# Packed small matmuls in the prologue and the channel gate, and the last image's convolutions in two parts, in a fused attention and convolution kernel

## The chip, the cores and the metric

The kernel runs on one core of a Trainium2 chip. The metric is the device time of one execution in microseconds (us). The core has five engines that run side by side and meet at semaphores: TensorE (PE in the profile; its weight loads are PEld), VectorE (DVE), ScalarE (ACT), GpSimd (POOL) and SyncE (SP, which here issues most DMA transfers). The kernel before takes 3579.54 us, the median of three runs (3570.65 to 3580.26).

## The reference

Two images x of 256 channels by 64 by 64 pixels, all in float32, go through two layers. Cut to what matters:

```python
# layer 0: full attention over 4096 tokens, 8 heads of 32 channels
m = resize(mask, (B, 1, 64, 64), "bilinear")
q, k, v = proj(Wq, bq) / sqrt(32), proj(Wk, bk), proj(Wv, bv)
fuse = softmax(q @ k.T) @ v                        # per image and head
hybrid = conv1x1(concat([x, fuse]), Wf, bf)
x = hybrid * m + x * (1 - m)

# layer 1
a = relu(x @ ca_w1 + ca_b1) @ ca_w2 + ca_b2        # channel gate: 256 -> 64 -> 256
x = x * sigmoid(a)
x = x + window_attention(x)                        # 8 by 8 windows, 4 heads of 64
x = shuffle_channels(x, 4)
y = relu(bn1(conv7x7(x, sa_w1, groups=64)))        # 256 -> 64 channels
y = bn2(conv7x7(y, sa_w2, groups=64))              # 64 -> 256 channels
out = x * sigmoid(y)
```

## The kernel before

**Prologue.** For every image and every chunk of 512 tokens (16 chunks in all), PE computes q, k and v, which go to DRAM. It also sums the squares of q and k per head. Their maxima give a bound on the scores, by which the kernel chooses at run time whether softmax may go without subtracting the row maximum ("arm a", the one that runs here) or not ("arm b"). Each sum of squares is a matmul with 32 columns of weights. These matmuls stand right behind the projection whose squares they sum:

```python
norms = ps1.tile([P, CH], F32, tag="av", name=f"nrm_{b}_{c}")
for i, (n, w, eng) in enumerate((("q", wq, 0), ("k", wk, 1))):
    s = psum2(f"{n}0_{b}_{c}")
    ...                                   # 4 matmuls of 128x128 weights by 512 tokens (L156)
    for g in range(KC):
        nc.vector.tensor_scalar_add(t[:, g, :], s[:, g, :], bt[:, g : g + 1])
        nc.scalar.activation(sq[:, g, :], s[:, g, :], AF.Square, bias=bt[:, g : g + 1])
    for g in range(KC):
        r = 64 * i + 32 * g
        nc.tensor.matmul(norms[r : r + 32, :], headsum, sq[:, g, :], start=True, stop=True)
...                                       # then v (L185) and the maximum of norms
```

GpSimd meanwhile builds banded weights for the two 7x7 convolutions in DRAM (`w1_s`, `w2_s`), zeroing them and then writing their diagonals.

**Attention loop.** It has 1024 slots: image, chunk of 512 queries, half of the heads, block of 128 keys. In each slot PE makes scores for four heads in four row tiles (L484), ACT takes the exponential (L492), DVE adds it to a running sum (L508) and PE multiplies by v in four column tiles (L506). The denominators (`dna`, L523) are four neighbouring column tiles too. Keys and values are loaded every four slots, two pieces ahead.

Once a chunk is done, its further path (fusion, channel gate, window attention) runs as a "stage" of 15 steps, one every fourth slot of the next chunk. The channel gate is two of those steps:

```python
for kc in range(KC):
    nc.tensor.matmul(s[0:CR, 0, :], cw1[:, kc, :], x1[:, kc, :], start=(kc == 0), stop=(kc == KC - 1))
gt = gp.tile([CR, CH], F32, tag="g", name=f"g{tag}")
nc.scalar.activation(gt, s[0:CR, 0, :], AF.Relu, bias=cb1)
yield
s = psum2(f"ca2{tag}")
for oc in range(KC):
    nc.tensor.matmul(s[:, oc, :], cw2[:, oc * P : (oc + 1) * P], gt, start=True, stop=True)
```

**Convolutions.** An image's convolutions start once its eighth chunk is stored in DRAM (`x_s`). The rows are cut into three overlapping blocks of 30; the partition dimension holds 4 channels x 30 rows. A unit is `UG = 4` channels of each of four quarters, so there are 16 units. All three blocks are side by side in one matmul: 3 x 64 = 192 columns. Per unit each convolution has 28 matmuls (two records each in the profile).

```python
conv_after = {(b, NCHUNK - 1): (0, 1, 2) for b in range(B)}
...
def load_w(u):                                     # banded weights, 448 KB each
    for ws, d, i in ((w1s, w1_s, 1), (w2s, w2_s, 2)):
        t = wsp.tile([P, 32, UW], F32, tag="w", name=f"w{i}{tag}_{u}")
        nc.sync.dma_start(t, d[u])
        ws[u] = t

def load_x(u):                                     # 4 loads per block
    if u >= NU:
        return
    x = xs[u] = xcs[u % len(xcs)]                  # four buffers
    for n, blk in enumerate(blocks):
        r = BLOCKS[blk][0]
        for q in range(4):
            ...
            nc.sync.dma_start(x[4 + q : 4 + 4 * RB : 4, n], x_s[b][r : r + RB, gs, :])
...
load_w(0)
load_w(1)
yield
for u in range(len(xcs)):
    load_x(u)
yield
conv1(0)
yield
for u in range(NU):
    conv1(u + 1)                                   # PE (L783), then Relu on ACT
    yield
    z = conv2(u)                                   # PE (L804), then sigmoid on ACT
    yield
    gate(u, z)                                     # DVE (L826), then stores
    if u + 2 < NU:
        load_w(u + 2)
    load_x(u + len(xcs))
    yield
```

The first image's convolutions run beside the second image's attention, one step every fourth slot (`if i % 4 == 2: run_convs()`). Those of the last image have nothing left to run beside; they make the tail. Stores there are shared between GpSimd's and ScalarE's queues.

Of the kernel before, what the change touches and what calls it, by code (L numbers as in the profile page):

```python
# [10 lines left out]
F32 = mybir.dt.float32  # L11
# [28 lines left out]
RB = 30  # L40
BLOCKS = ((0, 0, 24), (17, 24, 40), (34, 40, 64))
NG = C // 4
UG = 4
UQ = UG // 4
NU = NG // UG
UW = UG * KS
EPS = 1e-5
# [6 lines left out]
def conv_seq_kernel(ctx: ExitStack, tc: tile.TileContext, a, out):  # L54
# [24 lines left out]


    xcs, ycs = [], []
    for u in range(4):
        t = const.tile([P, len(BLOCKS), UG, WP], F32, name=f"xc{u}")
        nc.gpsimd.memset(t, 0.0)
        nc.gpsimd.memset(t[0:1], 1.0)
        xcs.append(t)
        t = const.tile([P, UQ, len(BLOCKS), WP], F32, name=f"yc{u}")
        nc.gpsimd.memset(t, 0.0)
        ycs.append(t)

# [32 lines left out]
    with (  # L123
# [19 lines left out]
        for b in range(B):  # L143
            src = a["x"][b].rearrange("(k p) h w -> p k (h w)", p=P)
            for c in range(NCHUNK):
                x = x0.tile([P, KC, CH], F32, tag="x", name=f"x0_{b}_{c}")
                nc.sync.dma_start(x, src[:, :, c * CH : (c + 1) * CH])
                norms = ps1.tile([P, CH], F32, tag="av", name=f"nrm_{b}_{c}")
                for i, (n, w, eng) in enumerate((("q", wq, 0), ("k", wk, 1))):
                    s = psum2(f"{n}0_{b}_{c}")  # L150
                    for g in range(KC):
                        for kc in range(KC):
                            rhs = x[:, kc, :]
                            if n == "q":
                                rhs = rhs.rearrange("p (r w c) -> p w r c", r=WS, w=NW)
                            nc.tensor.matmul(  # L156
                                s[:, g, :],
                                w[:, kc, g * P : (g + 1) * P],
                                rhs,
                                start=(kc == 0),  # L160
                                stop=(kc == KC - 1),
                            )
                    t = st0.tile([P, KC, CH], F32, tag=n, name=f"{n}st_{b}_{c}")
                    sq = st0.tile([P, KC, CH], F32, tag="sq", name=f"{n}sq_{b}_{c}")
                    bt = bias["b" + n]
                    for g in range(KC):
                        nc.vector.tensor_scalar_add(t[:, g, :], s[:, g, :], bt[:, g : g + 1])  # L167
                        nc.scalar.activation(
                            sq[:, g, :], s[:, g, :], AF.Square, bias=bt[:, g : g + 1]
                        )  # L170
                    for g in range(KC):
                        r = 64 * i + 32 * g
                        nc.tensor.matmul(
                            norms[r : r + 32, :], headsum, sq[:, g, :], start=True, stop=True
                        )
                    if n == "q":
                        nc.sync.dma_start(q_s[b, c], t.rearrange("p g n -> p (g n)"))
                    else:
                        for g in range(KC):
                            nc.sync.dma_start(k_s[b, g, c], t[:, g, :])  # L180
                s = psum2(f"v0_{b}_{c}")
                sv = s.rearrange("p a (t o) -> p (a t) o", t=2)
                for m in range(4):
                    for kc in range(KC):
                        nc.tensor.matmul(  # L185
                            sv[:, m, :],
                            x[:, kc, m * P : (m + 1) * P],
                            wv[:, kc, :],
                            start=(kc == 0),
                            stop=(kc == KC - 1),  # L190
                        )
                v = st0.tile([P, KC, 4, P], F32, tag="v", name=f"vst_{b}_{c}")
                nc.scalar.copy(
                    v.rearrange("p g m d -> p m g d"),
                    sv.rearrange("p m (g d) -> p m g d", g=KC),
                )
                for g in range(KC):
                    nc.sync.dma_start(v_s[b, g, c], v[:, g].rearrange("p m d -> p (m d)"))
                i = b * NCHUNK + c
                nc.vector.tensor_reduce(nm[:, i : i + 1], norms, AX.X, ALU.max)  # L200
# [19 lines left out]
    wo = load("out_w", [P, KC, C], a["out_w"].rearrange("(k p) o -> p k o", p=P), nc.scalar)  # L220
    bo = load("out_b", [P, KC], a["out_b"], nc.scalar)
    cw1 = load("ca_w1", [P, KC, CR], a["ca_w1"].rearrange("(k p) o -> p k o", p=P), nc.scalar)
    cb1 = load("ca_b1", [CR, 1], a["ca_b1"], nc.scalar)
    cw2 = load("ca_w2", [CR, C], a["ca_w2"], nc.scalar)
    cb2 = load("ca_b2", [P, KC], a["ca_b2"], nc.scalar)


# [51 lines left out]
        "bn2", bn2.rearrange("p h q (s k) -> p (h q) s k", k=2)  # L279
    )  # L280
    raw2 = cwp.tile([rows, 16, 4, KS], F32, name="raw2")
    m2 = cwp.tile([rows, NU, 4, UQ, KS], F32, name="m2")
    nc.gpsimd.memset(m2, 0.0)
    src = a["sa_w2"].rearrange("(h q j) k (y x) -> h k j y q x", h=2, j=4, y=KS)
    for i in range(4):
# [4 lines left out]
    for i in range(4):  # L290
        h, k = i % 2, i // 2
        v = sc2.rearrange("p (h q) k -> p h q k", h=2)[:, h, :, k]
        nc.vector.tensor_mul(
            m2[0:nd, :, i],
            raw2[0:nd, :, i, :].rearrange("p (u q) x -> p u q x", q=UQ),
            v[0:nd].rearrange("p (u q) -> p u q", q=UQ).unsqueeze(3).to_broadcast(
                [nd, NU, UQ, KS]
            ),
        )
        v = sh2.rearrange("p (h q) k -> p h q k", h=2)[:, h, :, k]  # L300
        nc.vector.tensor_copy(
            m2[32:36, :, i, :, PAD], v[32:36].rearrange("p (u q) -> p u q", q=UQ)
        )

    zero = cwp.tile([P, 32 * UW], F32, name="zero")
# [70 lines left out]
    def pipeline(arm, shifted, pools):  # L376
# [191 lines left out]
        def stage(b, c):  # L568
# [33 lines left out]
            if nxt[0] < B:  # L602
                load_x(*nxt)
            yield
            s = psum2(f"ca1{tag}")
            for kc in range(KC):
                nc.tensor.matmul(  # L607
                    s[0:CR, 0, :], cw1[:, kc, :], x1[:, kc, :], start=(kc == 0), stop=(kc == KC - 1)
                )
            gt = gp.tile([CR, CH], F32, tag="g", name=f"g{tag}")  # L610
            nc.scalar.activation(gt, s[0:CR, 0, :], AF.Relu, bias=cb1)
            yield
            s = psum2(f"ca2{tag}")
            for oc in range(KC):
                nc.tensor.matmul(  # L615
                    s[:, oc, :], cw2[:, oc * P : (oc + 1) * P], gt, start=True, stop=True
                )
            t = gp.tile([P, KC, CH], F32, tag="t", name=f"sg{tag}")
            for oc in range(KC):
                nc.scalar.activation(  # L620
                    t[:, oc, :], s[:, oc, :], AF.Tanh, bias=cb2[:, oc : oc + 1], scale=0.5
                )
            nc.scalar.activation(t, t, AF.Copy, bias=0.5, scale=0.5)
            u = wp.tile([P, KC, CH], F32, tag="u", name=f"u{tag}")
# [121 lines left out]
            if (b, c) in conv_after:  # L746
                convs.append(ahead.pop(0) if ahead else convolve(b, conv_after[b, c]))

        conv_after = {(b, NCHUNK - 1): (0, 1, 2) for b in range(B)}

        def convolve(b, blocks):
# [9 lines left out]
                    ws[u] = t  # L763

            def load_x(u):
                if u >= NU:
                    return
                x = xs[u] = xcs[u % len(xcs)]
                for n, blk in enumerate(blocks):
                    r = BLOCKS[blk][0]  # L770
                    for q in range(4):
# [3 lines left out]
            def conv1(u):  # L775
# [1 line left out]
                    return  # L777
                x, w = xs[u], w1s.pop(u).rearrange("p m (g d) -> p g d m", g=UG)
                s = psum2(f"c1{tag}_{u}")
                for q in range(UQ):  # L780
                    for d in range(KS):
                        for j in range(4):
                            nc.tensor.matmul(  # L783
# [6 lines left out]
                y = ys[u] = ycs[u % 2]  # L790
                nc.scalar.activation(  # L791
                    y[:, :, 0:nb, PAD : PAD + W],
                    s[:, 0:UQ, 0 : nb * W].rearrange("p q (n x) -> p q n x", n=nb),
                    AF.Relu,
                )

            def conv2(u):
                y, w = ys.pop(u), w2s.pop(u).rearrange("p m (i q d) -> p q d (m i)", q=UQ, i=4)
                tiles = [psum2(f"c2{tag}_{u}_{hh}") for hh in range(2)]
                for q in range(UQ):  # L800
                    for d in range(KS):
                        for j in range(4):
                            r = slice(32 * j, 32 * j + 32)
# [4 lines left out]
                                start=(d == 0),  # L808
                                stop=(d == KS - 1),
                            )  # L810
                z = cp.tile([P, UQ, 4, len(BLOCKS) * W], F32, tag="z", name=f"z{tag}_{u}")
                z = z[:, :, :, 0 : nb * W]
                for hh in range(2):
                    nc.scalar.activation(  # L814
                        z[:, :, 2 * hh : 2 * hh + 2, :],
                        tiles[hh][:, :, 0 : UQ * nb * W].rearrange("p j (q f) -> p q j f", q=UQ),
                        AF.Tanh,
                        scale=0.5,
                    )
# [3 lines left out]
            def gate(u, z):  # L823
# [5 lines left out]
                for n, blk in enumerate(blocks):  # L829
                    x0, r0, r1 = BLOCKS[blk]  # L830
                    for i in range(4):
                        p0, p1 = (4 * (r + 1 - x0) + i for r in (r0, r1))

                        eng = nc.scalar if b == B - 1 and i == 3 else nc.gpsimd
                        eng.dma_start(  # L835
                            dst[i, r0:r1, UG * u : UG * u + UG, :], z[p0 : p1 - 3 : 4, :, n, :]
                        )

            load_w(0)
            load_w(1)  # L840
            yield
            for u in range(len(xcs)):
                load_x(u)
            yield
            conv1(0)
            yield
            for u in range(NU):
# [4 lines left out]
                gate(u, z)  # L852
                if u + 2 < NU:
                    load_w(u + 2)
                load_x(u + len(xcs))
                yield

        def run_convs():
# [23 lines left out]
        for i, (b, c, g, m) in enumerate(slots):  # L882
# [14 lines left out]
            run_later()  # L897
            if i % 4 == 0:
                run_stages()
            if i % 4 == 2:  # L900
                run_convs()
        while stages or convs or later:
            now[0] += 1
# [89 lines left out]
```

## Time and profile before

| | |
|---|---|
| Time | 3579.54 us (3570.65 to 3580.26) |
| Span of the profiled execution | 3578.5 us |
| Prologue | 0 to about 256 us |
| Attention loop with stages, convolutions of image 0 beside it from 1877 us on | about 256 to 3290 us |
| Last chunk's stage | to 3350 us |
| Convolutions of image 1 | 3356 to 3578 us |

How to read the profile: a group of instructions is a line with engine, operation, output<-inputs, shapes and count; behind the bar come its busy time in us, the mean duration of one in ns, and the idle time of the engine just ahead of it with what ended that. Records that overlap are counted once in the busy time, so busy time over count can be far below the mean duration where several tiles of the array work at once. A matmul of float32 leaves two records. `32*128` ahead of a shape is the tile of the array in use (rows*columns). The answer by windows gives, for each stretch of time, PE's and PEld's busy time with the number of instructions, the granted clock, the DMA share and GB/s. In the timeline each row has its start, its duration, the engine, what ran, and in brackets the idle time ahead and its releaser. "SPq" rows are the issuing of transfers by SyncE.

### The profile page before, as it was taken

What the parts mean: (1) busy time and instruction counts of PE and PEld (TensorE: products, weight loads), DVE (VectorE), ACT (ScalarE), POOL (GpSimd) and SP (SyncE); (2) the same over time, 40 slices, a digit from 0 to 9 for tenths busy, and PEclk for the clock granted to TensorE, in tenths of its full rate; (3) what the DMA queues carried; (4) which work ended last, traced back from release to release, by engine and by line L of the source; (5) the groups of instructions that cost most, each with busy time, mean ns of one, the idle gap of its engine ahead of it and who ended that gap; (6) DMA issues with size and microseconds to landing.
All of it is one profiled execution on the core that took longest, in us unless ns stands there. A gap on an engine that the chain in (4) does not pass through costs nothing.

```text
span 3578.5 us, 57141 instructions
## 1 busy us (share of the span) xinstructions
PE 3307.4 (92%) x23690; PEld 1145.7 (32%) x23690; DVE 2718.2 (76%) x1775; ACT 2333.0 (65%) x2581; POOL 312.1 (9%) x543
## 2 busy tenths in 40 slices
PE   9999999999999999999998999999999999998565
PEld 3432222222222222223232443334322222222344
DVE  2229989898989898889987786887889898988100
ACT  2228777786868786777775676767677777775111
POOL 6400000000000000000000111121100000000044
PEclk9999999999999999999999999999999999999777
DMA  8942122121212121211223232332212121211143
GB/s 306 201 135 66 48 59 54 54 57 52 59 54 57 48 63 48 60 51 55 56 62 93 78 98 78 97 92 76 61 51 60 48 63 51 54 54 48 48 130 93
DMA packets 159438, 269.94 MB, mean 75 GB/s; under 512 B 41401, under 2 KB 56909, under 8 KB 159169
## 3 DMA queue, kind: packets, MB, share of 16 engines
q1 hardware_dynamic: 130976, 227.93, 22.1%
q0 software_dynamic: 19648, 34.71, 4.0%
q10 hardware_dynamic: 8544, 3.55, 0.4%
q8 instruction: 189, 3.10, 0.4%
q14 instruction: 81, 0.66, 0.1%
HBM read 208.49 MB, written 60.65 MB: 75 GB/s over the span
## 4 chain that ended last, share of the span: by engine, by line
PE 49%; DVE 18%; issue 17%; ACT 3%; SPq 3%; DMA 2%; POOL 0%; DVEq 0%; ACTq 0%; POOLq 0%
PE sa L484 20%; PE ava L506 16%; DVE suma L508 13%; PE qka L633 3%; PE c2a L804 3%; SPq L773 3%; PE c1a L783 2%; ACT ea L492 2%; PE opa L725 1%; PE vwa L650 1%; DVE rda L529 1%; PE ca2a L615 1%; PE ca1a L607 1%; PE oa L708 1%; DVE pbd L689 1%
## 5 line engine op out<-in xcount | busy, mean ns | idle before, releaser
L508 DVE TENSOR_TENSOR suma<-suma,ea 128x2048 f32<-128x2048 f32 x960 | 2199.9, 2292 | 312.9 <-ACT ea L492 235.5
L492 ACT ACTIVATE ea<-sa 128x1024 f32<-128x1024 f32 x2048 | 1985.2, 1023 | 444.5 <-PE sa L484 307.4
L484 PE MATMUL sa<-qa,ka 32*128 32x512 f32 x8192 | 1336.5, 649 | 88.4 <-ACT ea L492 41.3
L506 PE MATMUL ava<-ea,va 128*32 128x512 f32 x8192 | 1111.0, 614 | 0.0
L484 PEld LDWEIGHTS sa<-qa,ka 32*128 32x128 f32 x8192 | 434.1, 186 | 929.4 <-issue 494.4
L506 PEld LDWEIGHTS ava<-ea,va 128*32 128x32 f32 x8192 | 162.6, 109 | 793.5 <-issue 790.3
L835 POOL DMA_DIRECT2D out_dram<-za x336 | 187.6, 566 | 669.7 <-ACT ea L492 458.1
L740 POOL DMA_DIRECT2D xs<-xo x32 | 28.5, 895 | 2310.6 <-DVE xo L735 2309.2
L783 PE MATMUL c1a<-xc,w1a 128*32 128x192 f32 x1792 | 107.9, 406 | 84.7 <-DMA xc<-xs 25.1
L826 DVE TENSOR_TENSOR za<-za,xc 128x768 f32<-128x768 f32 x32 | 30.6, 957 | 199.2 <-ACT za L820 142.6
L633 PE MATMUL qka<-ua,qkv_w 128*128 128x512 f32 x256 | 130.5, 634 | 28.6 <-ACT qka L641 24.9
L783 PEld LDWEIGHTS c1a<-xc,w1a 128*32 128x32 f32 x1792 | 80.8, 151 | 114.2 <-issue 97.0
L804 PE MATMUL c2a<-yc,w2a 32*128 32x192 f32 x1792 | 116.3, 403 | 0.1
L804 PEld LDWEIGHTS c2a<-yc,w2a 32*128 32x128 f32 x1792 | 108.5, 321 | 20.5 <-issue 17.6
L641 ACT ACTIVATE qka<-qka,qkv_b 128x512 f32<-128x512 f32 x64 | 44.0, 687 | 108.8 <-PE qka L633 107.6
L791 ACT ACTIVATE yc<-c1a 128x192 f32<-128x192 f32 x32 | 10.6, 332 | 155.3 <-PE c1a L783 136.9
L529 DVE RECIPROCAL rda<-rda 128x512 f32<-128x512 f32 x32 | 107.1, 3346 | 2.8 <-ACT rda L526 2.8
L814 ACT ACTIVATE za<-c2a 128x384 f32<-128x384 f32 x64 | 27.9, 488 | 94.8 <-PE c2a L804 89.1
L508 DVE TENSOR_TENSOR suma<-ea,ea 128x2048 f32<-128x2048 f32 x32 | 73.1, 2285 | 18.3 <-ACT ea L492 18.3
L633 PEld LDWEIGHTS qka<-ua,qkv_w 128*128 128x128 f32 x256 | 44.8, 195 | 114.6 <-issue 57.9
L167 DVE TENSOR_SCALAR qst<-q,bq 128x512 f32<-128x512 f32 x32 | 24.0, 751 | 70.8 <-PE q L156 58.5
L725 PE MATMUL opa<-ota,out_w 128*128 128x512 f32 x128 | 63.5, 619 | 13.3 <-ACT ya L732 12.4
(124 smaller groups left out, 1634.7 us busy)
## 6 DMA issues: line engine op xcount, KB each, us to landing
ka<-ks SPq DMA_DIRECT2D x256, 256.0 KB
va<-vs SPq DMA_DIRECT2D x256, 256.0 KB
w1a<-w1s SPq DMA_DIRECT2D x32, 448.0 KB
w2a<-w2s SPq DMA_DIRECT2D x32, 448.0 KB
xc<-xs SPq DMA_DIRECT2D x384, 32.8 KB
xs<-xo POOLq DMA_DIRECT2D x32, 280.0 KB, 7.0
x<-in_x_dram SPq DMA_DIRECT2D x16, 512.0 KB
ks<-kst SPq DMA_DIRECT2D x32, 256.0 KB
```

Source lines behind the costliest of these rows:

```text
L484: nc.tensor.matmul(o, k[r, cols], q[r, g, :], start=True, stop=not shifted)
L492: nc.scalar.activation(e[:, 2 * hh : 2 * hh + 2, :], tiles[hh], AF.Exp, scale=SCALE0)
L506: nc.tensor.matmul(av[r, :], v[:, m % PB, r], e[:, j, :], start=start, stop=stop)
L508: nc.vector.tensor_add(total, first[0] if m == 1 else total, e)
L529: nc.vector.reciprocal(rd, rd)
L633: nc.tensor.matmul(s[:, j, :], wqkv[:, kc, o : o + P], u[:, kc, :], start=(kc == 0), stop=(kc == KC - 1),)
L641: nc.scalar.activation(qk[:, n, :], s[:, j, :], AF.Identity, bias=bqkv[:, n : n + 1])
L725: nc.tensor.matmul(s[:, oc, :], wo[:, kc, oc * P : (oc + 1) * P], ot[:, kc, :], start=(kc == 0), stop=(kc == KC - 1),)
L773: nc.sync.dma_start(x[4 + q : 4 + 4 * RB : 4, n], x_s[b][r : r + RB, gs, :])
L783: nc.tensor.matmul(s[32 * j : 32 * j + 32, q, 0 : nb * W], w[:, 4 * q + j, d, :], x[:, 0:nb, 4 * q + j, d : d + W], start=(d == 0), stop=( ...
L804: nc.tensor.matmul(tiles[j // 2][:, j % 2, q * nb * W : (q + 1) * nb * W], w[r, q, d], y[r, q, 0:nb, d : d + W], start=(d == 0), stop=(d = ...
L835: eng.dma_start(dst[i, r0:r1, UG * u : UG * u + UG, :], z[p0 : p1 - 3 : 4, :, n, :])
```

## The change

Three parts. The sums of squares are collected and issued as four neighbouring column tiles of 32, after the chunk's v projection. The channel gate works on two halves of the 512 tokens at once: its first matmul (64 output channels) in two column tiles, its second (64 input channels) in two row tiles, so that both halves of the array have work. And the convolutions are arranged anew, with the last image's split: the two upper row blocks start after chunk 5 and run beside the attention of the last chunk, with steps every second slot, and only the third block remains for the tail. In this arrangement a unit has 8 channels of each quarter (8 units), tiles have two buffers instead of four, and all stores of results go through GpSimd.

```diff
-UG = 4
-UQ = UG // 4
+UG = 8
...
-    for u in range(4):
+    for u in range(2):
         t = const.tile([P, len(BLOCKS), UG, WP], F32, name=f"xc{u}")
...
-                    for g in range(KC):
-                        r = 64 * i + 32 * g
-                        nc.tensor.matmul(
-                            norms[r : r + 32, :], headsum, sq[:, g, :], start=True, stop=True
-                        )
+                    sqs += [sq[:, g, :] for g in range(KC)]
...                                        # v projection
+                norms = ps1.tile([P, CH], F32, tag="av", name=f"nrm_{b}_{c}")
+                for i, sq in enumerate(sqs):
+                    nc.tensor.matmul(
+                        norms[32 * i : 32 * i + 32, :], headsum, sq, start=True, stop=True
+                    )
...
+            half = CH // 2
+            toks = [slice(half * h, half * h + half) for h in range(2)]
             s = psum2(f"ca1{tag}")
             for kc in range(KC):
-                nc.tensor.matmul(
-                    s[0:CR, 0, :], cw1[:, kc, :], x1[:, kc, :], start=(kc == 0), stop=(kc == KC - 1)
-                )
-            gt = gp.tile([CR, CH], F32, tag="g", name=f"g{tag}")
+                for h in range(2):
+                    nc.tensor.matmul(
+                        s[64 * h : 64 * h + 64, 0, 0:half],
+                        cw1[:, kc, :],
+                        x1[:, kc, toks[h]],
+                        ...
+                    )
+            gt = gp.tile([P, half], F32, tag="g", name=f"g{tag}")
...
             for oc in range(KC):
-                nc.tensor.matmul(
-                    s[:, oc, :], cw2[:, oc * P : (oc + 1) * P], gt, start=True, stop=True
-                )
+                for h in range(2):
+                    r = slice(64 * h, 64 * h + 64)
+                    nc.tensor.matmul(
+                        s[:, h, half * oc : half * oc + half],
+                        cw2[r, oc * P : (oc + 1) * P],
+                        gt[r, :],
+                        ...
+                    )
...
-        conv_after = {(b, NCHUNK - 1): (0, 1, 2) for b in range(B)}
+        conv_after = {(b, NCHUNK - 1): (0, 1, 2) for b in range(B - 1)}
+        conv_after[B - 1, 5] = (0, 1)
+        conv_after[B - 1, NCHUNK - 1] = (2,)
...
-                x = xs[u] = xcs[u % len(xcs)]
+                x = xs[u] = xcs[u % 2]
...
-                        eng = nc.scalar if b == B - 1 and i == 3 else nc.gpsimd
-                        eng.dma_start(
+                        nc.gpsimd.dma_start(
...
-            for u in range(len(xcs)):
-                load_x(u)
+            load_x(0)
+            load_x(1)
...
                 if u + 2 < NU:
                     load_w(u + 2)
-                load_x(u + len(xcs))
+                    load_x(u + 2)
...
-            if i % 4 == 2:
+            if i % 4 == 2 or (i % 4 == 0 and (b, c) >= (B - 1, 6)):
                 run_convs()
```

## What the change was predicted to do

> **What bounds the kernel now.** I read the page first: busy times, then the slices.
>
> ```profile
> PE 3307.4 (92%) x23690; PEld 1145.7 (32%) x23690; DVE 2718.2 (76%) x1775; ACT 2333.0 (65%) x2581; POOL 312.1 (9%) x543
> ...
> PE   9999999999999999999998999999999999998565
> ...
> DVE  2229989898989898889987786887889898988100
> ...
> PEclk9999999999999999999999999999999999999777
> ```
>
> A slice is 89.5 us. There are three stages: a prologue of projections (3 slices), where PE is full and DVE at 2; the attention loop, where PE is full and DVE nearly so; and a tail (the last 2.5 slices), where nothing is full and PE's clock reads 7. The change touches each, so I price each apart. The groups of instructions, shapes kept apart, give the costs in question:
>
> ```profile
> L804 PE MATMUL c2a<-yc,w2a 32*128 32x192 f32 x1792 | 116.3, 403 | 0.1
> L783 PE MATMUL c1a<-xc,w1a 128*32 128x192 f32 x1792 | 107.9, 406 | 84.7 <-DMA xc<-xs 25.1 <-issue 19.7 <-DMA out_dram<-za 14.1
> L523 PE MATMUL dna<-suma,ones 128*32 128x512 f32 x256 | 34.9, 614 | 16.8 <-DVE ewa L680 8.5 <-DVE suma L508 8.3
> L173 PE MATMUL nrm<-ksq,headsum 128*32 128x512 f32 x64 | 33.5, 605 | 0.0
> L615 PE MATMUL ca2a<-ga,ca_w 64*128 64x512 f32 x64 | 31.7, 615 | 0.8 <-ACT ga L611 0.8
> L607 PE MATMUL ca1a<-x1a,ca_w 128*64 128x512 f32 x64 | 31.1, 605 | 1.9 <-DVE x1a L596 1.9
> ```
>
> A matmul leaves two records. Divide busy time (of overlapping records, counted once) by count: `nrm` 523 ns a record, `dna` 136 ns. Both have 32 columns of weights and 512 of tokens; `dna` is issued as four neighbouring column tiles, `nrm` one at a time between other matmuls.
>
> For the loop, I count score records in stretches of time; a step of the loop ("slot") has eight. First 400 us in which the first image's convolutions run beside it, then 200 us without:
>
> ```profile
> 2050.00:2150.00 100.00, 41.46 (x256) 13.81 (x256) 1.00 0.32 93
> 2150.00:2250.00 100.00, 37.26 (x224) 11.87 (x224) 1.00 0.27 84
> 2250.00:2350.00 100.00, 42.20 (x256) 13.92 (x256) 1.00 0.34 92
> 2350.00:2450.00 100.00, 37.25 (x232) 12.07 (x232) 1.00 0.30 91
> ...
> 2800.00:3000.00 200.00, 88.17 (x552) 28.37 (x552) 0.99 0.20 55
> ```
>
> 968/8 = 121 slots in 400 us are 3.31 us each; 69 in 200 us are 2.90. So these convolutions cost 0.41 us x 204 slots = 84 us, though they hold PE for 97.7 us (57.9 + 39.8, the two lines alone). The waits of PE name one wait in it of 15.0 us, for keys stuck behind 48 tile loads. Hence only some 69 us are PE work that shows; the loop's small PE gaps swallow 28 us, 0.14 us a slot.
>
> Then the timeline: the reload of input tiles in the loop, and one unit of the tail.
>
> ```profile
> 2202.04 0.95 DVE L826 TENSOR_TENSOR za<-za,xc 128x768 f32<-128x768 f32 x1
> ...
> 2203.01 10.22 SPq L773 DMA_DIRECT2D xc<-xs  x12
> ...
> 2214.16 2.50 PE L783 MATMUL c1a<-xc,w1a 128*32 128x192 f32 x56
> ```
>
> ```profile
> 3424.88 3.84 PE L783 MATMUL c1a<-xc,w1a 128*32 128x192 f32 x56 [3.83 <-DMA w1a<-w1s]
> ...
> 3428.65 3.58 PE L804 MATMUL c2a<-yc,w2a 32*128 32x192 f32 x56
> ...
> 3434.04 0.96 DVE L826 TENSOR_TENSOR za<-za,xc 128x768 f32<-128x768 f32 x1 [10.22 <-ACT za L820]
> ...
> 3435.48 10.52 SPq L773 DMA_DIRECT2D xc<-xs  x12
> 3438.32 3.61 PEld L783 LDWEIGHTS c1a<-xc,w1a 128*32 128x32 f32 x56 [6.34 <-issue]
> ```
>
> The tail's first convolution starts at 3356.06 and the span ends at 3578.5: 222 us for 16 units, about 12.2 each. SyncE needs 0.86 us per load, 14 loads a unit: the tail is held by issuing loads and by the chain PE, ACT, DVE, load, PE, not by arithmetic. In the loop a reload ends only just before the next first convolution, 12 us later. Before, that reload is for four units on, so nobody waits. That matters below.
>
> **What the Trainium skill says.** (1) "TensorEngine Tiling (Array Packing)", Key Properties: different tiles work in parallel, and a change of tiling mode drains the array. The trace agrees: 136 against 523 ns a record. (2) "TensorE: Matmul & The Clock Gate", Part 1: about 3.4 us of idleness halves the clock, about as much work restores it. It agrees: the same 56 records take 2.50 us in the loop and up to 4.71 us in the tail, while the second convolution right behind takes 3.6 us in both. (3) The same page, Part 2, step-by-step: loading weights takes time by the number of columns. It agrees: PEld is busy 108.5 us over the second convolution's 1792 loads of 128 columns, 60 ns each, and its matmul records come every 64 ns (3.58 us for 56). Narrower images will not make it much shorter. (4) "DMA: Bandwidth & Descriptors", Issuing engines are not separate DMA queues: issue time is usually small against the transfer. This trace differs: twelve issues take 10.2 us, the last lands some 2.3 us later.
>
> **The change, part by part.**
>
> *Sums of squares.* A lone `nrm` matmul holds PE from 117.58 to 118.56, 0.98 us; four are 3.9 us of a chunk's 15.0 us (q bursts start at 112.34 and 127.35). In the changed order all four stand together after the v projections, so they should cost as `dna`, 8 x 136 ns = 1.1 us; k pairs are no longer split, which saves a little more. 3.1 us x 16 chunks = **-50 us**. ACT's squares are ready, as v takes 3.7 us.
>
> *Channel gate.* 1.94 + 1.98 us of PE per stage (31.1/16, 31.7/16) become half, two tiles side by side at 256 tokens: about 1.0 + 1.1. 1.8 us x 16 = 29, nearly all in the loop: **-27 us**.
>
> *First image.* Units twice as large, half as many; the same PE work. 27 steps (108 slots) instead of 51 (204) swallow 15 us instead of 28: +13. Only 24 loads at the start: the 15 us wait for keys should go, -13. But now there are two tile buffers, not four: a unit's reload starts after gating and is needed one step (4 slots) later. From the end of the slot's products: gate 2.8 us (twice as wide), twelve issues 10.3, landing 2.4 = 15.5; PE arrives after four slots and a stage step, 9.2 + 2.3 = 11.5. It waits 4 us, six times: +24. Sum **+24 us**.
>
> *Last image, two blocks moved into the loop.* 8 units of 112 + 112 records, 128 columns, in 27 steps (54 slots). First convolution: 178 ns per four records at 192 columns, some 125 at 128: 3.5 us. Second, nearly held by its weights: 50 to 60 ns a record, 6.2 us. 9.7 x 8 = 77, of which the 54 slots swallow 7. Steps come every two slots here: reload 2.5 + 8 x 0.86 + 2.4 = 11.8, plus up to 1 us behind weights twice as large; PE arrives after 5.5. It waits 7 us, six times, less at the start: +42. **+112 us**.
>
> *Tail.* Only the third block, 64 columns, 8 units, four loads of tiles and two of weights each. The first c1 starts when it did (it waits for the last chunk's rows). A unit: c1 cold 4 us, c2 5.5, ACT and DVE 2, four issues 3.2, landing 2.5 = 17.2 (two buffers make it a closed loop; 1.8 MB of weights per 17 us is 107 GB/s, below the 129 moved now). First two units 12.5, six more 103, last c2 5.5, outputs and end 15 (the end after the last issue is 11 now): 136 us instead of 222. **-86 us**.
>
> Sum: -50 - 27 + 24 + 112 - 86 = -27 us; 3579.5 - 27 = **3552 us**.
>
> **Rivals.** (a) *The reloads are hidden*: SyncE runs ahead, or stages space the steps. Then the 66 us of waits fall away: about 3487. For it: before, PE hardly waits for tiles in the loop. Against: that is with four buffers, and SyncE's issue rate is measured. (b) *The new wait is worse*: tile loads queue behind 1.8 MB of weights and keys behind tile loads, 4 to 6 us more per unit: about 3610. For it: the 15 us key wait. (c) *The prologue is bound by transfers once PE is faster*: the windows give a DMA share of about 1.0 from 50 to 150 us. Against: PE waits for no chunk now, the band writes have half as many descriptors, and a chunk's 2 MB in 12 us is 175 GB/s of 378 reached. It would give back up to 25 us: 3577.
>
> **Range and chances.** Prologue and gate are measured costs of like instructions, good to 10 us; the tail to 15; the loop waits to 40. Together 8 in 10 lie between 3505 and 3605. Two per cent faster means below 3508, which needs most of (a): 0.14. Two per cent slower means above 3651, beyond (b): 0.03. The rest, 0.83, is within.
>
> **What would show it.** `nrm` near 136 ns a record and the prologue about 50 us shorter; `ca1a`, `ca2a` near half; PE waits for tiles in the loop of 4 and 7 us, a dozen in all; tail about 136 us from first c1, units of 17 us. Wrong if PE never waits for tiles in the loop (then faster), or if the second convolution at 64 columns takes half of 60 ns a record (tail shorter by 20 us), or if the prologue keeps its length.

## The result, and the profile after

The changed kernel takes 3612.43 us (median of four runs, 3607.25 to 3626.37) against 3579.9 us: 1.010 times as long, with a 95% interval of 1.0065 to 1.0136. A gain of 27 us had been predicted; it lost 32.5 (the two profiled executions lie 27.0 apart). The page of its profiled execution (span 3605.5 us), the same rows as before:

```profile
PE 3314.2 (92%) x25610; PEld 1229.2 (34%) x25610; DVE 2715.6 (75%) x1767; ACT 2323.7 (64%) x2549; POOL 229.5 (6%) x377
...
PE   9999999999999999999999898999999999779865
...
DVE  3369989898989898989875665889999898445610
...
PEclk9999999999999999999999999999999999899975
```

Read the DVE row. The loop starts earlier (a 6 in the third slice), but there is a dip to 5 and 6 where the first image's convolutions run, and a second one, 445, where the last image's now run beside the last chunk. The tail is shorter. Cut at the same points of the work (the loads of queries, which SyncE issues once per chunk, the last products and the tail's first convolution), the two profiled executions differ like this:

| Stretch | before, us | after, us | difference | predicted |
|---|---|---|---|---|
| prologue, to the first load of queries | 251.6 | 207.9 | -43.7 | -50 |
| loop without convolutions | 1556.6 | 1538.5 | -18.1 | -15 |
| four chunks with the first image's convolutions | 836.0 | 877.2 | +41.1 | +17 |
| two chunks without | 368.6 | 364.5 | -4.1 | -3 |
| the rest of the loop, with two blocks of the last image | 270.7 | 406.1 | +135.4 | +110 |
| last stage | 72.6 | 73.7 | +1.1 | 0 |
| tail, from its first convolution | 222.4 | 137.7 | -84.7 | -86 |
| sum | | | +27.0 | -27 |

(The predicted 27 us for the gate are spread over the loop's rows by chunks.) The two rows in which convolutions run beside the loop are 24 and 25 us off; the prologue is 6 off. The groups for the operations concerned, shapes kept apart:

```profile
L827 PE MATMUL c2a<-yc,w2a 32*128 32x192 f32 x896 | 58.0, 410 | 0.0
L827 PE MATMUL c2a<-yc,w2a 32*128 32x64 f32 x896 | 58.0, 436 | 1.4 <-issue 1.4
L827 PE MATMUL c2a<-yc,w2a 32*128 32x128 f32 x896 | 57.0, 405 | 0.0
L806 PE MATMUL c1a<-xc,w1a 128*32 128x192 f32 x896 | 47.2, 376 | 31.2 <-DMA xc<-xs 27.5 <-issue 3.7
L806 PE MATMUL c1a<-xc,w1a 128*32 128x128 f32 x896 | 37.3, 342 | 43.1 <-DMA xc<-xs 43.1
...
L806 PE MATMUL c1a<-xc,w1a 128*32 128x64 f32 x896 | 24.7, 303 | 53.9 <-DMA xc<-xs 53.9
L190 PE MATMUL nrm<-ksq,headsum 128*32 128x512 f32 x64 | 21.0, 621 | 3.9 <-ACT ksq L167 3.8
...
L630 PE MATMUL ca2a<-ga,ca_w 64*128 64x256 f32 x128 | 18.7, 412 | 0.6 <-ACT ga L624 0.6
...
L190 PE MATMUL nrm<-qsq,headsum 128*32 128x512 f32 x64 | 17.9, 604 | 0.0
L616 PE MATMUL ca1a<-x1a,ca_w 128*64 128x256 f32 x128 | 17.6, 393 | 2.3 <-DVE x1a L601 2.3
```

Two things are to be seen. The second convolution is busy for the same 57 to 58 us at 192, 128 and 64 columns: 64 to 65 ns a record at all three widths. And the first convolution waits for its tiles: 31.2 us for the first image, 43.1 for the two blocks in the loop, 53.9 in the tail. Predicted were 24, 42 and (in units of 17 us) 7.7 per unit. So in sum the waits came about as foreseen. One by one they did not: the first image's lay between 0.8 and 9.7 us, where six of 4 had been worked out, and the last chunk's between 1.7 and 10.5, where there should have been six of 7. How one looks in the timeline (start, duration, engine, line, and in brackets the idle time):

```profile
3191.70 1.22 DVE L849 TENSOR_TENSOR za<-za,xc 128x1024 f32<-128x1024 f32 x1
3192.95 6.45 SPq L796 DMA_DIRECT2D xc<-xs  x8
...
3201.12 5.87 PE L806 MATMUL c1a<-xc,w1a 128*32 128x128 f32 x112 [5.04 <-DMA xc<-xs]
```

Gating frees the buffer at 3192.9, eight loads are issued until 3199.4, and PE starts 1.7 us later, when the last has landed. The convolution then takes 5.87 us. The next one waits less, and this is the difference:

```profile
3234.31 3.31 PE L806 MATMUL c1a<-xc,w1a 128*32 128x128 f32 x112 [1.72 <-DMA xc<-xs]
```

The same 112 records take 3.31 us after a wait of 1.7 us. The windows of these two convolutions show the granted clock, 0.54 in the first and 1.00 in the second (columns: stretch, its length, busy time of PE with count, clock, DMA share, GB/s):

```profile
3201.12:3206.99 5.87, 5.87 (x116) 0.54 0.23 82
3234.31:3237.62 3.31, 3.31 (x116) 1.00 0.14 48
```

The slow clock that the prediction knew from the tail is at work in the loop as well.

### The profile page after: what moved, and what is told of

Read it like the earlier page. It is cut to its first block, busy times and chain, and to the rows that moved or that the text cites. A ratio compares the mean times of both kernels' runs of the same rounds, so it can differ in the third digit from the quotient of the medians.

```text
span 3605.5 us, 60338 instructions
## 1 busy us (share of the span) xinstructions
PE 3314.2 (92%) x25610; PEld 1229.2 (34%) x25610; DVE 2715.6 (75%) x1767; ACT 2323.7 (64%) x2549; POOL 229.5 (6%) x377
## 5 line engine op out<-in xcount | busy, mean ns | idle before, releaser
L489 PE MATMUL sa<-qa,ka 32*128 32x512 f32 x8192 | 1354.0, 651 | 72.0 <-ACT ea L497 39.6
L806 PE MATMUL c1a<-xc,w1a 128*32 128x192 f32 (+2 forms) x2688 | 109.2, 340 | 128.2 <-DMA xc<-xs 124.5
L827 PE MATMUL c2a<-yc,w2a 32*128 32x192 f32 (+2 forms) x2688 | 173.0, 417 | 1.4 <-issue 1.4
L827 PEld LDWEIGHTS c2a<-yc,w2a 32*128 32x128 f32 x2688 | 167.9, 336 | 16.3 <-issue 13.0
L856 POOL DMA_DIRECT2D out_dram<-za x192 | 112.4, 593 | 751.0 <-ACT ea L497 502.7
L806 PEld LDWEIGHTS c1a<-xc,w1a 128*32 128x32 f32 x2688 | 99.4, 157 | 147.0 <-issue 140.3
L814 ACT ACTIVATE yc<-c1a 128x384 f32<-128x384 f32 (+2 forms) x24 | 9.3, 387 | 214.0 <-PE c1a L806 214.0
L849 DVE TENSOR_TENSOR za<-za,xc 128x1536 f32<-128x1536 f32 (+2 forms) x24 | 29.3, 1222 | 132.4 <-ACT za L843 132.3
L837 ACT ACTIVATE za<-c2a 128x768 f32<-128x768 f32 (+2 forms) x48 | 26.3, 594 | 157.5 <-PE c2a L827 157.3
```

The lines of the kernel that those rows point to most:

```text
L489: nc.tensor.matmul(o, k[r, cols], q[r, g, :], start=True, stop=not shifted)
L806: nc.tensor.matmul(s[32 * j : 32 * j + 32, q, 0 : nb * W], w[:, 4 * q + j, d, :], x[:, 0:nb, 4 * q + j, d : d + W], start=(d == 0), stop=( ...
L827: nc.tensor.matmul(tiles[j // 2][:, j % 2, q * nb * W : (q + 1) * nb * W], w[r, q, d], y[r, q, 0:nb, d : d + W], start=(d == 0), stop=(d = ...
L856: nc.gpsimd.dma_start(dst[i, r0:r1, UG * u : UG * u + UG, :], z[p0 : p1 - 3 : 4, :, n, :])
```

## Experiments

Times are medians; the ratio to the kernel before is in brackets with its interval. Stretches are those of the table, from the profiled execution.

**More room for tiles.** Does the loss come from the waits?

```diff
+    xbuf = const.tile([P, 2 * len(BLOCKS), UG, WP], F32, name="xc")   # same memory, cut by blocks
+            depth = min(3, 6 // nb)
...
+                if u >= NU:
+                    return
-                x = xs[u] = xcs[u % 2]
+                k = nb * (u % depth)
+                x = xs[u] = xbuf[:, k : k + nb]
...
             conv1(0)
+            if depth == 3:
+                load_x(2)
...
-                    load_x(u + 2)
+                load_x(u + depth)
                 yield
+                if depth == 2:
+                    yield
```

> The changed kernel, but no convolution is to wait for its tiles: for the last image the same tile memory is cut into three buffers (two blocks in the loop, one in the tail), loads one unit earlier; for the first image one empty step follows each gating, so that a reload has eight slots, not four. Theory W, waits for tiles and the slow clock after them are what the prediction missed: PE's waits for tiles in the loop fall from 74 us to under 15; the first image's stretch shrinks by some 40 us, the last chunk by some 50, the tail from 138 to about 107; in all about 3480 us. Theory L, the long convolution steps themselves starve the other engines and the waits only fill time that is lost anyway: the two stretches in the loop shrink by under 35 us together; about 3540.

Measured: 3494.41 us (0.9757, 0.9732 to 0.9782). The windows of the first image's stretch and of the rest of the loop, the changed kernel first, then this one (columns: stretch, its length, busy time of PE, PEld, DVE, ACT and POOL with counts, clock, DMA share, GB/s):

```profile
1746.00:2623.50 877.50, 818.53 (x6692) 310.23 (x6696) 668.91 (x417) 576.95 (x625) 63.37 (x104) 0.96 0.26 76
2988.00:3394.10 406.10, 354.26 (x3648) 169.33 (x3640) 251.80 (x153) 223.29 (x252) 40.23 (x68) 0.94 0.30 97
```

```profile
1756.70:2584.90 828.20, 801.47 (x6692) 303.15 (x6688) 668.32 (x417) 576.85 (x625) 63.48 (x104) 0.99 0.27 80
2954.70:3326.30 371.60, 348.38 (x3648) 164.30 (x3640) 251.95 (x153) 223.41 (x252) 40.23 (x68) 0.96 0.34 106
```

The same matmuls, 49 and 34.5 us less, and the tail fell from 137.7 to 95.8. Theory W holds, though the last chunk gained less than its 50 us; theory L had allowed under 35 us for both stretches. PE's waits for tiles in the loop fell from 74.3 to 15.8 us (14.5 of them in the last chunk). In the first image's stretch 30 us of waits gone made 49 us: the first convolution itself fell from 47.2 to 38.4 us, and PE's other work there by another 8.2 (818.5 - 47.2 against 801.5 - 38.4). Here a wait cost PE more than its length. The empty step also spreads the first image's convolutions over more slots; what that gave by itself was not tried.

**Both small parts on the kernel before.** Is the loss in the convolutions alone?

```diff
 # before.py
-  (sums of squares behind each projection)
+  (four neighbouring column tiles behind v, as in the change)
-  (channel gate on 512 tokens)
+  (channel gate on two halves, as in the change)
```

> The kernel before with both small parts of the change (sums of squares as four neighbouring tiles, channel gate on halves), its own convolutions kept. If the loss lies in the convolutions alone: 44 us less in the prologue and 3.2 us less per chunk, about 3487 us. If the small parts cost something later: above 3520.

Measured: 3535.48 us (0.9879, 0.9851 to 0.9908). The time lies in the second branch, but not for its reason: the profile shows no new loss later on, the parts saved less, 44 us instead of some 93. The prologue shrank by 32 us (251.6 to 219.5), not 44, and the loop without convolutions by 6 (1556.6 to 1550.3). The waits in the prologue, this kernel and then the changed one:

```profile
ACT vst L195 <- DMA vs<-vst: 27.9, 8, 5.4
...
DVE qst L167 <- DMA qs<-qst: 22.0, 4, 6.1
```

```profile
DVE qst L166 <- DMA qs<-qst: 7.6, 1, 7.6
```

The bias additions wait for q's buffer to be stored. This kernel still builds its banded weights in 16 units, with twice as many writes of half the size as the changed kernel's 8; in its window from 100 to 150 us the DMA share is 1.06 at 205 GB/s, in the changed kernel's 0.95 at 279. So with PE faster this prologue waits for stores, and the changed kernel's, with the larger unit, is 12 us shorter; the prediction had named the halved descriptors, but only as a point against rival (c). That it is the number of writes was not tried by itself.

**The gate alone**, on the kernel before (the second hunk of the last diff).

> The kernel before with the channel gate on halves only. If a stage saves just the PE time of the gate, 1.65 us: 27 us less, 3552. If it saves what the chunks of the changed kernel show, 3.2 us: about 48 us less, 3530.

Measured: 3564.53 us (0.9965, 0.9949 to 0.998), 15 us less (by the interval 7 to 18): below the PE time it saves.

**The gate undone**, in the changed kernel:

```diff
-  (channel gate on two halves)
+  (channel gate on 512 tokens, as before)
```

> The changed kernel with the channel gate as before. If the gate's PE time is what counts: 27 us slower, 3640. If the loop away from the convolutions does not follow PE's time, as the gate alone in the kernel before suggests (15 us): between 5 and 18 us slower, about 3625.

Measured: 3626.8 us (1.0131, 1.0104 to 1.0157), 14 us more than the changed kernel, but its interval overlaps that kernel's (1.0065 to 1.0136), so this difference alone is not clear of noise. It agrees with the 15 us above. The gate's PE time fell by (31.1 + 31.7) - (17.6 + 18.7) = 26.5.

**All at the end again**, everything else as changed:

```diff
-        conv_after[B - 1, 5] = (0, 1)
-        conv_after[B - 1, NCHUNK - 1] = (2,)
...
-            if i % 4 == 2 or (i % 4 == 0 and (b, c) >= (B - 1, 6)):
+            if i % 4 == 2:
```

> The changed kernel with all three blocks of the last image at the end again (units of eight channels, two tile buffers kept). Theory S, the split pays the second convolution's weight loads twice and so costs more in the loop than it saves: the last chunk shrinks by some 135 us, the tail grows from 138 to about 255 (30 us a unit: both convolutions 13, ACT and DVE 5, twelve issues 10, landing 2.5); about 3588. If the split itself is sound and only something else costs: the tail takes back more than the loop gives, above 3630.

Measured: 3572.85 us (0.9974, 0.9959 to 0.9988), 40 us less than the changed kernel. The rest of the loop took 271.2 us, so the two blocks had cost 134.9 there; the tail took 232.2 us, 94.5 more (255 had been expected for it). Theory S holds: what the split takes off the end is less than what it puts in. Its waits by the profile:

```profile
PE c1a L804 <- DMA xc<-xs: 141.2, 14, 16.9
```

141 us of waiting for tiles are left, most of it in the tail, with two buffers, so the split was not the only cost.

**All at the end, three full tile buffers.** The two findings together:

```diff
-    for u in range(2):
+    for u in range(3):
         t = const.tile([P, len(BLOCKS), UG, WP], F32, name=f"xc{u}")
...
-                x = xs[u] = xcs[u % 2]
+                x = xs[u] = xcs[u % 3]          # loads three units ahead
...
-            gt = gp.tile([P, half], F32, tag="g", name=f"g{tag}")
+            gt = gp.tile([P, WS, H // 2 + 2], F32, tag="mv", name=f"g{tag}")   # memory for it
+            gt = gt.rearrange("p r w -> p (r w)")[:, 0:half]
```

(Arm b, which does not run, gets one output buffer instead of two, to fit.)

> All three blocks of the last image at the end, units of eight channels, three full tile buffers, loads three units ahead (the memory comes from letting the gate's hidden tile share a place with a mask tile). Theory S and W together, split paid twice and waits for tiles: no waits in the loop (first image's stretch about 830 us as with the extra step), last chunk 271 us, tail from first convolution of 8 units at 16 us (12 us of PE and of issuing, 3.1 MB of transfers at 190 GB/s) plus 15, 145 us: about 3445 us, under both kernels. Rival, the tail is bound by transfers at the 130 GB/s that the kernel before reached there: 24 us a unit, tail 205 us, about 3505.

Measured: 3438.08 us (0.9612, 0.9583 to 0.9641), faster than both kernels. The first image's stretch took 832.1 us, the rest of the loop 271.2, the tail 149.8. The tail's first convolutions:

```profile
3342.65 4.85 PE L809 MATMUL c1a<-xc,w1a 128*32 128x192 f32 x112
3362.96 7.16 PE L809 MATMUL c1a<-xc,w1a 128*32 128x192 f32 x112 [8.39 <-DMA w1a<-w1s]
3377.13 4.83 PE L809 MATMUL c1a<-xc,w1a 128*32 128x192 f32 x112
```

Tiles are there in time; what is waited for in every second unit or so is now the weights. The clock shows again: 4.85 us without a wait, 7.16 after one of 8.39.

## Why the prediction was wrong

Its measure of the parts was mostly right; it failed in the two terms of the loop in which convolutions run. Both take a wait of PE at its length alone, without the slow clock behind it. Both also lean on gaps of the loop that swallow 0.14 us a slot, and this rests on a misreading: the 15.0 us wait for keys were taken off the 84 us, although the 400 us from which the 84 were worked out (2050 to 2450) do not hold that wait. In the kernel before it ended at 1929:

```profile
1929.06 2.09 PE L484 MATMUL sa<-qa,ka 32*128 32x512 f32 x8 [15.04 <-DMA ka<-ks]
```

Read rightly, the gaps swallowed 97.7 - 84 = 14 us, not 28: 0.07 us a slot.

- **Sums of squares, -50: measured -43.7.** A group of four (eight records, whose lines overlap each other in the list above) took 1.0 us, as `dna` does, and a chunk 11.5 us instead of 15.0, a little better than worked out:

```profile
67.50 0.62 PE L190 MATMUL nrm<-qsq,headsum 128*32 128x512 f32 x2
67.97 0.60 PE L190 MATMUL nrm<-ksq,headsum 128*32 128x512 f32 x2
68.50 3.70 PE L155 MATMUL q<-x,WqT 128*128 128x512 f32 x8
```

How much of the fall from 523 ns a record is the sharing of the array and how much the grouping by tiling mode, no run separates. But one chunk, from 80.01 to 99.53 us, took 19.5: the squares were late, because DVE waited for a store. That is rival (c), which had been given up to 25 us; it took 8. In the profiled executions with the gate undone and with three full tile buffers, whose sums of squares are the same, the prologue took 201.2 and 201.4 us, the full 50 less. The timeline row of the late chunk, in which the second half of the four waits for ACT:

```profile
96.18 1.19 PE L190 MATMUL nrm<-ksq,headsum 128*32 128x512 f32 x2 [3.52 <-ACT ksq L167]
```

- **Channel gate, -27: some -15.** PE's time was right (26.5), the step "nearly all in the loop" was not. Chunks of identical code took 180.9 us in most cases in the changed kernel's execution and 183.5 to 185.8 in that of the kernel with everything at the end. Two chunks of the changed kernel, in the columns used above:

```profile
653.87:834.83 180.96, 174.01 (x1228) 0.99 0.20 56
1379.53:1565.35 185.82, 177.21 (x1228) 0.97 0.20 55
```

In the second, one wait for an exponential is 2.6 us instead of 0.9, and the same matmuls take 3.2 us longer, at a lower granted clock. Between chunks with the same wait and clock, the gate does show its PE time of 1.65 us: with the gate undone such chunks took 182.6 and 187.5 us. So its saving mixes with a variation three times as large. In the table's rows this error is small (18.1 + 4.1 against 18), as that execution fell on the favourable side.
- **First image, +24: about 24 us more.** The waits were sized at 24 and measured 31.2 (+7). The failed step is "gate, issue, landing against arrival" taken as the whole cost of a wait: the first convolution after it ran at the slow clock (47.2 against 39.8, +7.4), and the scores and products around it lost another 8.2, as the first experiment shows. These three make 23. Of the other two terms, the 15 us of key wait are gone: the changed kernel has no wait of PE for keys. The 13 us less swallowed come from the misreading; at 0.07 us a slot they are 7. What the gaps swallowed in this stretch of the changed kernel was not measured by itself: with the waits away the stretch (828) is 8 us shorter than in the kernel before, which fits 13 (-15 + 13 - 7 for the gate is -9) better than 7, but in that run the steps are spread over more slots.
- **Two blocks in the loop, +112: measured +135.** The failed steps, term by term, are "50 to 60 ns a record, 6.2 us": it is 64 ns, 57.0 us for the eight units against 49.6 (+7); "3.5 us" for the first convolution: 37.3 against 28 (+9), of which at least 5 are the slow clock, as it is 31.9 with fewer waits; and "of which the 54 slots swallow 7", 4 when read rightly. Little was swallowed: 94.3 us of PE and 43.1 of waits are 137.4, and the stretch without convolutions (271.2) is 134.9 shorter. The waits themselves, 42 predicted, were 43.1, by some luck: they were seven of very unlike length, and the first, at the start, was 9.3 us, where less than 7 had been put.
- **Tail, -86: measured -84.7.** First convolution to end took 137.7 us against 136, a unit 17.3 against 17.2. Errors cancel here: the second convolution took 7.1 us, not 5.5, the first 3.2, not 4, and the wait was 7.2, not 7.7:

```profile
3507.72 2.99 PE L806 MATMUL c1a<-xc,w1a 128*32 128x64 f32 x112 [7.20 <-DMA xc<-xs]
3510.64 7.09 PE L827 MATMUL c2a<-yc,w2a 32*128 32x64 f32 x112
3524.94 3.22 PE L806 MATMUL c1a<-xc,w1a 128*32 128x64 f32 x112 [7.21 <-DMA xc<-xs]
```

Of the rivals, (a), hidden reloads, did not happen, but its price is telling: it was put at 66 us for the loop, and taking most of the waits away gave 84 there. (b), transfers queued behind larger weights, at 4 to 6 us more per unit, did not happen either: the waits in the loop came to 74.3 us in sum against 66. The result came near (b)'s figure for another reason. The range was too narrow, as all the loop's errors went the same way.

What stays open: what sets the wait and the clock by which a chunk takes 181 or 184 to 186 us, and with it how much of the gate's saving is kept; what the gaps of the loop swallow beside the first image; and how much of the 12 us in the prologue is owed to the number of writes.

## What to carry to other kernels

Work that is moved beside a full engine has to be priced at its whole busy time there; gaps that seem free swallow little of it. A matmul whose weights change every time may not get cheaper when it streams fewer columns, so cutting the stream in two can pay it twice: compare shapes before splitting. And price a wait of TensorE at its length and the slow clock that can follow it: in the changed kernel's loop every wait of 3.7 us or more ahead of a first convolution had a slowed one behind it, and one of the four between 1.7 and 2.5 us. If a buffer is freed one step before it is refilled and needed, one more buffer, or one more step in between, is worth trying first.

## What had not been expected of the hardware

The second convolution (32 rows, 128 columns of weights, new weights for each matmul) takes 64 to 65 ns per record at 64, 128 and 192 streamed columns alike: 58.0, 57.0 and 58.0 us for 896 records. The first (128 rows, 32 columns) does shrink: 31.9 us at 128 and 38.4 at 192 for 896 records in the first experiment, with few waits. In the changed kernel's loop its 112 records of 128 columns took 3.3 us after waits of 1.7 and 2.5 us, 4.8 after one of 4.3, and 5.5 to 5.9 after waits of 5 to 10.5. A short wait is no warrant: 112 records of 192 columns took 4.83 us after a wait of 1.91 us and 6.50 after one of 1.83, at granted clocks of 1.00 and 0.74.
